# Attention between image columns and rows with the key projection folded into the query, the output bias moved to GpSimd, and image 1's group statistics taken inside image 0's attention

## The chip, the cores and the metric

The kernel runs on one core of one Trainium2 chip. The metric is the device time of one launch in microseconds. The profile is of one execution.

## What is computed

The input x has two images of 256 x 256 positions with 128 channels, in float32. Two layers follow each other, and each adds its result to x. This case concerns layer 0:

```
g   = groupnorm(x)                       # 32 groups of 4 channels, statistics over the whole image
q   = g Wq' + bq ;  k = g Wk' + bk ;  v1 = g Wv1' + bv1 ;  v2 = g Wv2' + bv2
a   = softmax(q k' / sqrt(128))          # queries: column l of the image; keys: row l
x1  = x + ((a v2) * v1) Wo' + bo
```

Attention is separate for each l from 0 to 255: the queries (and v1) are the 256 positions of column l, the keys (and v2) those of row l, and the result belongs to column l. Layer 1 takes x1, normalises it in the same way, and runs a gated depthwise convolution and a selective scan with 256 inner channels and 16 states over all 65,536 positions. It is not touched by the change, and it takes most of the time.

## The kernel before

The kernel has four stages, one after the other.

1. **Start (lines 69 to 184).** Small weights are loaded through SP's queue, transposed by TensorE and copied by ACT.
2. **Statistics (L225 to L243).** For each image, eight pieces of 4 MB (`TT = 64` positions per partition, `NT = 8`) come in through SP's queue into three buffers `xt`; for each piece DVE issues 32 `bn_stats`, one per channel group, over 256 elements. `group_stats` (L187) combines them: 32 `bn_aggr` over the pieces, two small matmuls, and a few small DVE operations and one GpSimd power give the scale `rs` and shift `sh` of each channel. Both images are done before attention begins.
3. **Attention (L255 to L400).** For each image, 16 groups (`NG`) of 16 values of l (`LG`) are loaded, one group ahead of its use: `xc` holds columns for the queries' side, `xr` rows for the keys' side. One call of `attention` handles two values of l (`LQ = 2`), 512 positions, so a group has 8 calls, an image 128, the kernel 256. A call transposes and normalises `xnc` and `xnr` (TensorE, then ACT), computes `q`, `k`, `v1`, `v2` (TensorE; biases added by DVE or ACT on the way out of PSUM), and then for each of its two l: scores `s_ps` (two matmuls), maximum `mx` and `nmx` (DVE), `e` with its sum `den` (ACT), `rden` and `a` (DVE), the transposes `aT_ps`, their copy `aT` (ACT for the first, DVE for the second), and `c_ps` (TensorE). At the end DVE forms `ct`, TensorE the output `o_ps`, and DVE adds `xc` to it into the group's `x1g`. The output's bias is a matmul of one row, `ones_row` x `bo_row`, that opens the accumulation in `o_ps`. After a group, DVE issues 32 `bn_stats` on `x1g` for layer 1's statistics, and POOL's queue stores `x1g` to `x1` in HBM. After an image, `group_stats` combines them.
4. **Scan stage (L402 onwards).** Layer 1, whose order of work is written out by hand in slots.

In the first three stages the order of instructions on each engine is set by the tile framework's scheduler when the program is built[...]. All of `xnc_ps`, `xnr_ps`, `q_ps`, `k_ps`, `v1_ps`, `v2_ps` and `o_ps` take turns in three PSUM buffers:

```
ps_mm = actx.enter_context(tc.tile_pool(name="at_mm", bufs=3, space=PSUM))
```

[...]

Of the kernel before, what the change touches and what calls it, by code (L numbers as in the profile page):

```python
# [8 lines left out]
F32 = mybir.dt.float32  # L9
AF = mybir.ActivationFunctionType  # L10
ALU = mybir.AluOpType
# [4 lines left out]
P = 128  # L16
# [5 lines left out]
def attn_then_ssm_kernel(  # L22
# [26 lines left out]
    nc = tc.nc  # L49
    B, H, W, C = x.shape  # L50
    L = H * W
    G = 32
    CG = C // G
# [4 lines left out]
    TB = 512  # L58
# [10 lines left out]
    def column(name, src):  # L69

        t = const.tile([P, 1], F32, name=name)
        nc.sync.dma_start(out=t, in_=src.rearrange("(p o) -> p o", o=1))
        return t
# [11 lines left out]
    neg_half = const.tile([P, TB // P], F32, name="neg_half")  # L85
    nc.vector.memset(neg_half, -0.5)

    ones_row = const0.tile([1, P], F32, name="ones_row")
    nc.vector.memset(ones_row, 1.0)

    wq = const0.tile([P, P], F32, name="wq")
    wk = const0.tile([P, P], F32, name="wk")
    wv1 = const0.tile([P, P], F32, name="wv1")
    wv2 = const0.tile([P, P], F32, name="wv2")
    wo = const0.tile([P, P], F32, name="wo")
    bq_c = column("bq_c", bq)
    bk_c = column("bk_c", bk)
    bv1_c = column("bv1_c", bv1)  # L100
    bv2_c = column("bv2_c", bv2)
    bo_row = const0.tile([1, TB // P, C], F32, name="bo_row")
    nc.sync.dma_start(out=bo_row, in_=bo.partition_broadcast(TB // P).unsqueeze(0))

    cb_c = columns("cb_c", conv_b)
    dtb_c = columns("dtb_c", dt_b.rearrange("o d -> (o d)"))
# [24 lines left out]
    with tc.tile_pool(name="prep", bufs=1) as prep, tc.tile_pool(  # L131
        name="prep2", bufs=3
    ) as prep2, tc.tile_pool(name="prep_ps", bufs=4, space=PSUM) as prep_ps:
        inp = prep.tile([P, 2 * NH, P], F32, name="inp")
        nc.sync.dma_start(out=inp, in_=in_proj_w.rearrange("(k p) c -> p k c", p=P))
        cw = prep.tile([P, NH, 9], F32, name="cw")
        nc.sync.dma_start(out=cw, in_=conv_w.rearrange("(h p) o i j -> p h (o i j)", p=P))
        outp = prep.tile([P, DI], F32, name="outp")
        nc.sync.dma_start(out=outp, in_=out_proj_w)
        xpw = prep.tile([64, DI], F32, name="xpw")  # L140
        nc.vector.memset(xpw, 0.0)
        nc.sync.dma_start(out=xpw[0:DR, :], in_=x_proj_w[0, 0:DR, :])
        nc.sync.dma_start(out=xpw[32:64, :], in_=x_proj_w[0, DR : DR + 2 * NS, :])
        dtw = prep.tile([P, NH, DR], F32, name="dtw")
        nc.sync.dma_start(out=dtw, in_=dt_w[0].rearrange("(h p) r -> p h r", p=P))
        alog_d = dram.tile([CQ, SR, NCG, NSG], F32, name="alog_d")
        for g in range(NCG):
            for m in range(NSG):
                nc.sync.dma_start(
                    out=alog_d[:, :, g, m],  # L150
                    in_=A_logs[g * CQ : (g + 1) * CQ, m * SR : (m + 1) * SR],
                )
        alog = prep.tile([P, NCG, NSG], F32, name="alog")
        nc.sync.dma_start(out=alog, in_=alog_d.rearrange("c r g m -> (c r) g m"))
        a_pos = prep.tile([P, NCG, NSG], F32, name="a_pos")
        nc.scalar.activation(a_pos, alog, AF.Exp)
        nc.vector.tensor_scalar(a_neg, a_pos, -1.0, None, ALU.mult)

        def transposed(dst, src, n):
            pt = prep_ps.tile([P, P], F32, name="pt")  # L160
            m = dst.shape[0]
            nc.tensor.transpose(pt[0:m, 0:n], src, ident[0:n, 0:n])
            nc.scalar.copy(dst, pt[0:m, 0:n])

        for dst, src in ((wq, Wq), (wk, Wk), (wv1, Wv1), (wv2, Wv2), (wo, Wo)):
            wl = prep2.tile([P, P], F32, name="wl")
            nc.sync.dma_start(out=wl, in_=src)
            transposed(dst, wl, P)
        for h in range(NH):
            for tap in range(9):  # L170
                wt = prep2.tile([P, P], F32, name="wt")
                nc.vector.tensor_scalar(wt, inp[:, h, :], cw[:, h, tap : tap + 1], None, ALU.mult)
                transposed(w_tap[:, h, tap, :], wt, P)
            transposed(w_z[:, h, :], inp[:, NH + h, :], P)
            transposed(w_out[:, h, :], outp[:, h * P : (h + 1) * P], P)
            transposed(w_xp[:, h, :], xpw[:, h * P : (h + 1) * P], 64)
            transposed(w_dt[:, h, :], dtw[:, h, :], P)
            nc.vector.tensor_scalar(d_diag[:, h, :], ident, ds_c[:, h : h + 1], None, ALU.mult)
# [43 lines left out]
        nc.vector.tensor_scalar(sh, cs[:, 0:1], rs, -1.0, ALU.mult, ALU.mult)  # L222
        return rs, sh

    gn0 = []  # L225
    TT = 64
    NT = L // (P * TT)
    with tc.tile_pool(name="st", bufs=2) as stp, tc.tile_pool(
        name="st_x", bufs=3
    ) as stx, tc.tile_pool(name="st_ps", bufs=2, space=PSUM) as st_ps:  # L230
        for b in range(B):
            stats = stp.tile([P, G, NT, 6], F32, name="stats")
            for k in range(NT):
                xt = stx.tile([P, TT, C], F32, name="xt")
                nc.sync.dma_start(
                    out=xt,
                    in_=x_tok[b, k * P * TT : (k + 1) * P * TT, :].rearrange(
                        "(p t) c -> p t c", p=P
                    ),
                )  # L240
                for g in range(G):
                    nc.vector.bn_stats(stats[:, g, k, :], xt[:, :, g * CG : (g + 1) * CG])
            gn0.append(group_stats(stats, stp, st_ps, f"0_{b}"))  # L243

# [4 lines left out]
    NG = W // LG  # L251
    LQ = TB // H
    KT = H // P
    gn1 = []
    with ExitStack() as actx:  # L255
        ap = actx.enter_context(tc.tile_pool(name="at", bufs=2))
        ps_mm = actx.enter_context(tc.tile_pool(name="at_mm", bufs=3, space=PSUM))
        ps_s = actx.enter_context(tc.tile_pool(name="at_s", bufs=2, space=PSUM))
        ps_t = actx.enter_context(tc.tile_pool(name="at_t", bufs=2, space=PSUM))
# [11 lines left out]
        def attention(xc, xr, x1g, q, rs, sh):  # L271
# [3 lines left out]
            xnr = normalised("xnr", [xr[:, l, j, :] for l in ls for j in range(KT)], rs, sh)  # L275

            q_ps = ps_mm.tile([P, TB], F32, name="q_ps", tag="mm")
            nc.tensor.matmul(q_ps, wq, xnc, start=True, stop=True)
            qT = ap.tile([P, TB], F32, name="qT")
            nc.vector.tensor_scalar(qT, q_ps, bq_c, None, ALU.add)  # L280
            k_ps = ps_mm.tile([P, TB], F32, name="k_ps", tag="mm")
            nc.tensor.matmul(k_ps, wk, xnr, start=True, stop=True)
            kT = ap.tile([P, TB], F32, name="kT")
            nc.scalar.activation(kT, k_ps, AF.Identity, bias=bk_c)
            v1_ps = ps_mm.tile([P, TB], F32, name="v1_ps", tag="mm")
            nc.tensor.matmul(v1_ps, wv1, xnc, start=True, stop=True)
            v1 = ap.tile([P, TB], F32, name="v1")
# [12 lines left out]
            for r in range(LQ):  # L300
                own = slice(r * H, (r + 1) * H)
                s_ps = ps_s.tile([P, KT, H], F32, name="s_ps")
                for i in range(KT):
                    nc.tensor.matmul(
                        s_ps[:, i, :],
                        qT[:, r * H + i * P : r * H + (i + 1) * P],
                        kT[:, own],
                        start=True,
                        stop=True,
                    )  # L310
# [41 lines left out]
            ct = ap.tile([P, TB], F32, name="ct")  # L352
            nc.vector.scalar_tensor_tensor(ct, c_ps, bv2_c, v1, ALU.add, ALU.mult)
            o_ps = ps_mm.tile([P, LQ, KT, C], F32, name="o_ps", tag="mm")
            nc.tensor.matmul(o_ps, ones_row, bo_row, start=True, stop=False)
            for r in range(LQ):
                for i in range(KT):
                    t = r * H + i * P
                    nc.tensor.matmul(
                        o_ps[:, r, i, :],  # L360
                        ct[:, t : t + P],
                        wo,
                        start=False,
                        stop=(r == LQ - 1 and i == KT - 1),
                    )
            nc.vector.tensor_tensor(  # L366
                x1g[:, :, q * LQ : (q + 1) * LQ, :],
                o_ps.rearrange("p r i c -> p i r c"),
                xc[:, :, q * LQ : (q + 1) * LQ, :],
                ALU.add,  # L370
            )

        for b in range(B):
            rs, sh = gn0[b]
            stats1 = ap.tile([P, G, NG, 6], F32, name="stats1")

            def load(g):
                ls = slice(g * LG, (g + 1) * LG)
# [12 lines left out]
            for g in range(NG):  # L391
                nxt = load(g + 1) if g + 1 < NG else None
                x1g = ap.tile([P, KT, LG, C], F32, name="x1g")
                for q in range(LG // LQ):
                    attention(*got, x1g, q, rs, sh)
                for gr in range(G):
                    nc.vector.bn_stats(stats1[:, gr, g, :], x1g[:, :, :, gr * CG : (gr + 1) * CG])
                nc.gpsimd.dma_start(  # L398
                    out=x1[b][:, g * LG : (g + 1) * LG, :].rearrange("(i p) l c -> p i l c", p=P),
                    in_=x1g,  # L400
                )
                got = nxt  # L402
            gn1.append(group_stats(stats1, ap, ps_mm, f"1_{b}"))

    front.close()
# [509 lines left out]
```

## Time and profile before

| what | value |
|---|---|
| median of 3 runs | 18009.35 us (18005.79 to 18027.44) |
| profiled execution | 17985.75 us, span 17983.9 us |
| start and statistics | 0 to 240 us |
| attention, image 0 | 253 to 1772 us |
| attention, image 1 | 1800 to 3322 us |
| scan stage, with its prologue | 3345 us to the end |
| busy over the span | PE 79%, DVE 85%, ACT 62%, POOL 75% |
| mean granted TensorE clock | 0.906 |

Shares over the whole span say little here, since more than four fifths of it are the scan stage. The change lies in the first 3,345 us, so each of its steps is read in a window of its own. A matmul of float32 appears as two records[...] with the exception of transposes, which have one.

### The profile page before, as it was taken

To read this page: it belongs to the slowest core of one execution; us is meant where nothing else is said; L and a number is where in the kernel's file an instruction comes from. 1 tells how busy PE (TensorE), PEld (TensorE's weight loads), DVE (VectorE), ACT (ScalarE), POOL (GpSimd) and SP (SyncE) were. 2 spreads that over 40 slices of the span, in tenths; PEclk is the share of its full clock that TensorE was granted. 3 is DMA by queue.
4 is the path that set the end of the run, shared out by engine and by line. 5 is a ranking of instruction groups with operands and counts; after the bars stand their busy time and mean duration, and the time that the engine had idled before them with its cause. 6 is when DMAs were issued, how large, how long until landed. Compare 5 with 4: busy or idle time off the path is not lost. (4 is left out here: it accounts for less than half of the span.)

```text
span 17983.9 us, 178799 instructions
## 1 busy us (share of the span) xinstructions
PE 14262.3 (79%) x56375; PEld 6982.8 (39%) x56375; DVE 15218.5 (85%) x12864; ACT 11112.9 (62%) x19870; POOL 13400.1 (75%) x7084
## 2 busy tenths in 40 slices
PE   4999999777777777777777777777777777777776
PEld 3666666433333333333333333333333333333333
DVE  6555555499999999999999999999999999999998
ACT  2444444466666666666666666666666666666665
POOL 0000000299999999999999999999999999999998
PEclk7999999888899999999999888889888899999887
DMA  4122122266666666666666666666666666666664
GB/s 190 65 71 71 57 71 71 92 220 218 218 221 220 221 221 221 221 221 221 220 220 221 221 219 219 220 220 221 221 220 218 219 221 220 220 220 220 220 219 170
DMA packets 1426641, 3452.04 MB, mean 192 GB/s; under 512 B 119788, under 2 KB 710936, under 8 KB 1407256
## 3 DMA queue, kind: packets, MB, share of 16 engines
q1 hardware_dynamic: 1416984, 3373.49, 54.7%
q0 software_dynamic: 8704, 67.11, 0.9%
q8 instruction: 443, 7.26, 0.2%
q14 instruction: 510, 4.18, 0.1%
HBM read 2752.28 MB, written 687.88 MB: 191 GB/s over the span
## 5 line engine op out<-in xcount | busy, mean ns | idle before, releaser
L787 POOL TENSOR_TENSOR hb<-du_r,bb 128x1024 f32<-128x1024 f32 x4096 | 9566.1, 2360 | 0.0
L794 DVE TENSOR_TENSOR_SCAN da<-da,state,hb 128x1024 f32<-128x1024 f32 x2944 | 6912.4, 2348 | 1064.3 <-ACT da L779 749.3
L779 ACT ACTIVATE da<-delta_r,a_neg 128x1024 f32<-128x1024 f32 x4096 | 4575.5, 1117 | 1155.2 <-DVE hb L794 1086.4
L504 PE MATMUL u_ps<-xn,w_tap 128*128 128x512 f32 x9216 | 4218.6, 603 | 332.3 <-ACT sz L540 242.8
L806 DVE TENSOR_TENSOR yc<-da,cc 128x1024 f32<-128x1024 f32 x2944 | 3605.0, 1225 | 254.2 <-DVE da L794 4.6
L806 POOL TENSOR_TENSOR yc<-hb,cc 128x1024 f32<-128x1024 f32 x1152 | 2714.5, 2356 | 818.9 <-issue 411.9
L794 DVE TENSOR_TENSOR_SCAN hb<-da,state,hb 128x1024 f32<-128x1024 f32 x1152 | 2697.4, 2342 | 15.6 <-ACT da L779 15.3
L826 PE MATMUL y<-yc,sel 128*32 128x512 f32 x16384 | 2469.9, 671 | 280.5 <-POOL yc L806 274.1
L504 PEld LDWEIGHTS u_ps<-xn,w_tap 128*128 128x128 f32 x9216 | 1710.5, 192 | 2348.3 <-issue 1764.8
L398 POOL DMA_DIRECT2D x<-x1g x32 | 23.2, 725 | 3035.0 <-DVE x1g L366 3035.0
L656 PE MATMUL yt<-centre,ys 128*128 128x256 f32 x4096 | 1226.0, 452 | 798.1 <-ACT ob L726 797.0
L799 ACT COPY state<-da 128x1 f32<-128x1 f32 x2944 | 461.2, 157 | 2209.2 <-DVE yc L806 2206.7
L656 PEld LDWEIGHTS yt<-centre,ys 128*128 128x128 f32 x4096 | 895.4, 226 | 1200.8 <-ACT ob L726 992.0
L691 PE MATMUL yd<-ident,yn 128*128 128x128 f32 x2048 | 382.0, 317 | 1126.6 <-ACT yn L680 955.7
L826 PEld LDWEIGHTS y<-yc,sel 128*32 128x32 f32 x16384 | 477.0, 115 | 1973.1 <-issue 1263.9
L552 PE MATMUL xd_ps<-xs,w_xp 128*64 128x512 f32 x1024 | 602.2, 720 | 314.9 <-ACT state L799 174.4
L691 PEld LDWEIGHTS yd<-ident,yn 128*128 128x128 f32 x2048 | 273.3, 160 | 1407.7 <-ACT yn L680 993.9
L570 PE MATMUL dt_ps<-xd,w_dt 8*128 8x512 f32 x1024 | 608.5, 675 | 191.0 <-ACT xd L565 184.1
L515 ACT ACTIVATE xs<-u_ps,cb_c 128x512 f32<-128x512 f32 x512 | 349.6, 683 | 617.8 <-PE u_ps L504 342.5
L318 ACT ACTIVATE e<-s_ps,nmx 128x256 f32<-128x256 f32 x1024 | 472.5, 473 | 355.1 <-DVE nmx L314 354.6
L598 POOL TENSOR_TENSOR xs<-delta,xs 128x1024 f32<-128x1024 f32 x256 | 603.7, 2358 | 40.5 <-ACT delta L589 39.2
L716 PEld LDWEIGHTS o_ps<-w_out,yg 128*128 128x128 f32 x4096 | 604.7, 212 | 35.6
(134 smaller groups left out, 18144.6 us busy)
## 6 DMA issues: line engine op xcount, KB each, us to landing
bb<-bc_d SPq DMA_DIRECT2D x1024, 512.0 KB, 4.2
cc<-bc_d SPq DMA_DIRECT2D x1024, 512.0 KB, 5.2
delta_r<-delta_d SPq DMA_DIRECT2D x1024, 512.0 KB, 5.6
du_r<-du_d SPq DMA_DIRECT2D x1024, 512.0 KB, 4.1
xs_d<-xs SPq DMA_DIRECT2D x128, 1024.0 KB, 3.9
xr<-xs_d SPq DMA_DIRECT2D x256, 512.0 KB, 5.1
delta_d<-delta SPq DMA_DIRECT2D x128, 1024.0 KB, 7.2
du_d<-xs SPq DMA_DIRECT2D x256, 512.0 KB, 3.1
```

Of the source, the lines that this page charges most:

```text
L504: nc.tensor.matmul(o["u"], w_tap[:, h, 3 * dy + dx, :], o["xn"][:, i * RB + dy : i * RB + dy + RB, dx : dx + W], start=(dy == 0 and dx == ...
L552: nc.tensor.matmul(o["xd_ps"], w_xp[:, h, :], o["xs"][:, h, i * TB : (i + 1) * TB], start=(h == 0), stop=(h == NH - 1),)
L570: nc.tensor.matmul(o["dt"], w_dt[:, h, :], o["xd"][0:DR, i * TB : (i + 1) * TB], start=True, stop=True,)
L598: nc.gpsimd.tensor_tensor(du, o["delta"][:, h, :], du, ALU.mult)
L656: nc.tensor.matmul(o["yt"][:, j, :], ys[k, h][:, t0 + j * P : t0 + (j + 1) * P], centre[:, (1 - h) * P : (1 - h) * P + DI], start=(h == 0) ...
L691: nc.tensor.transpose(o["yd"][:, h, j * P : (j + 1) * P], o["yn"][:, j, h * P : (h + 1) * P], ident,)
L716: nc.tensor.matmul(o["o"][:, j, :], o["yg"][:, h, j * P : (j + 1) * P], w_out[:, h, :], start=False, stop=(j == WT - 1 and h == NH - 1),)
L779: nc.scalar.activation(da, spreads["delta", k, h, q], AF.Exp, scale=a_neg[:, g, m : m + 1])
L787: nc.gpsimd.tensor_tensor(hb, spreads["du", k, h, q], repeats["bb", k, h, m], ALU.mult)
L794: nc.vector.tensor_tensor_scan(u["h"], u["da"], u["hb"], st, ALU.mult, ALU.add)
L806: eng.tensor_tensor(u["yc"], u["h"], repeats["cc", k, h, m], ALU.mult)
L826: nc.tensor.matmul(y[q * CQ : (q + 1) * CQ, cols], sel, units[t + q]["yc"][:, cols], start=False, stop=(m == NSG - 1),)
```

## The change

- **One matrix for the scores.** The scores are q k' = (g Wq' + bq)(g Wk' + bk)'. What `bk` adds is the same for all keys of a query, so softmax drops it. The rest is (g Wq'Wk + bq Wk) g'. The kernel computes `wqk` = Wq'Wk and `bqk` = Wk'bq once, at the start. The matmul and the eviction of `k` go; the scores' moving operand is `xnr` itself.
- **Output bias.** The one-row matmul goes. GpSimd writes `xc + bo` into `x1g`, with `bo_all` being the bias on all partitions, and DVE then adds `o_ps` to it in place.
- **Statistics.** Only image 0's are taken before attention, in 16 pieces of 2 MB (`TT = 32`, six buffers). Image 1's pieces are issued by `piece_stats` inside the loop over image 0's groups, into one buffer of a new pool `at1`; `group_stats` for image 1 follows that loop.

```diff
-    wq = const0.tile([P, P], F32, name="wq")
-    wk = const0.tile([P, P], F32, name="wk")
+    wqk = const0.tile([P, P], F32, name="wqk")
+    bqk = const0.tile([P, 1], F32, name="bqk")
...
-    bo_row = const0.tile([1, TB // P, C], F32, name="bo_row")
-    nc.sync.dma_start(out=bo_row, in_=bo.partition_broadcast(TB // P).unsqueeze(0))
+    bo_all = const0.tile([P, C], F32, name="bo_all")
+    nc.sync.dma_start(out=bo_all, in_=bo.partition_broadcast(P))
...
-        for dst, src in ((wq, Wq), (wk, Wk), (wv1, Wv1), (wv2, Wv2), (wo, Wo)):
+        wqr = prep.tile([P, P], F32, name="wqr")
+        nc.sync.dma_start(out=wqr, in_=Wq)
+        wkr = prep.tile([P, P], F32, name="wkr")
+        nc.sync.dma_start(out=wkr, in_=Wk)
+        qk_ps = prep_ps.tile([P, P], F32, name="qk_ps", tag="pt")
+        nc.tensor.matmul(qk_ps, wqr, wkr, start=True, stop=True)
+        nc.scalar.copy(wqk, qk_ps)
+        bqk_ps = prep_ps.tile([P, P], F32, name="bqk_ps", tag="pt")
+        nc.tensor.matmul(bqk_ps[:, 0:1], wkr, bq_c, start=True, stop=True)
+        nc.scalar.copy(bqk, bqk_ps[:, 0:1])
+        for dst, src in ((wv1, Wv1), (wv2, Wv2), (wo, Wo)):
...
-    TT = 64
+    TT = 32
     NT = L // (P * TT)
-    with tc.tile_pool(name="st", bufs=2) as stp, tc.tile_pool(
-        name="st_x", bufs=3
+    def piece_stats(b, k, stats, pool):
+        xt = pool.tile([P, TT, C], F32, name="xt")
+        nc.sync.dma_start(
+            out=xt,
+            in_=x_tok[b, k * P * TT : (k + 1) * P * TT, :].rearrange("(p t) c -> p t c", p=P),
+        )
+        for g in range(G):
+            nc.vector.bn_stats(stats[:, g, k, :], xt[:, :, g * CG : (g + 1) * CG])
+    with tc.tile_pool(name="st", bufs=1) as stp, tc.tile_pool(
+        name="st_x", bufs=6
     ) as stx, tc.tile_pool(name="st_ps", bufs=2, space=PSUM) as st_ps:
...
+        stats = stp.tile([P, G, NT, 6], F32, name="stats")
+        for k in range(NT):
+            piece_stats(0, k, stats, stx)
+        gn0[0] = group_stats(stats, stp, st_ps, "0_0")
...
-            nc.tensor.matmul(q_ps, wq, xnc, start=True, stop=True)
+            nc.tensor.matmul(q_ps, wqk, xnc, start=True, stop=True)
-            nc.vector.tensor_scalar(qT, q_ps, bq_c, None, ALU.add)
-            k_ps = ps_mm.tile([P, TB], F32, name="k_ps", tag="mm")
-            nc.tensor.matmul(k_ps, wk, xnr, start=True, stop=True)
-            kT = ap.tile([P, TB], F32, name="kT")
-            nc.scalar.activation(kT, k_ps, AF.Identity, bias=bk_c)
+            nc.vector.tensor_scalar(qT, q_ps, bqk, None, ALU.add)
...
-                        kT[:, own],
+                        xnr[:, own],
...
-            nc.tensor.matmul(o_ps, ones_row, bo_row, start=True, stop=False)
...
-                        start=False,
-                        stop=(r == LQ - 1 and i == KT - 1),
+                        o_ps[:, r, i, :], ct[:, t : t + P], wo, start=True, stop=True
...
-            nc.vector.tensor_tensor(
-                x1g[:, :, q * LQ : (q + 1) * LQ, :],
-                o_ps.rearrange("p r i c -> p i r c"),
+            to = x1g[:, :, q * LQ : (q + 1) * LQ, :]
+            nc.gpsimd.tensor_tensor(
+                to,
                 xc[:, :, q * LQ : (q + 1) * LQ, :],
+                bo_all.unsqueeze(1).unsqueeze(1).to_broadcast([P, KT, LQ, C]),
                 ALU.add,
             )
+            nc.vector.tensor_tensor(to, o_ps.rearrange("p r i c -> p i r c"), to, ALU.add)
...
+                if b + 1 < B:
+                    for k in range(g * NT // NG, (g + 1) * NT // NG):
+                        piece_stats(b + 1, k, stats0, ap1)
                 got = nxt
+            if b + 1 < B:
+                gn0[b + 1] = group_stats(stats0, ap, ps_mm, f"0_{b + 1}")
```

More of the change, by code (lines that the diff above doesn't have):

```diff
@@ L86, in attn_then_ssm_kernel @@
     nc.vector.memset(neg_half, -0.5)
-    ones_row = const0.tile([1, P], F32, name="ones_row")
-    nc.vector.memset(ones_row, 1.0)
-    wq = const0.tile([P, P], F32, name="wq")
-    wk = const0.tile([P, P], F32, name="wk")
+    wqk = const0.tile([P, P], F32, name="wqk")
+    bqk = const0.tile([P, 1], F32, name="bqk")
     wv1 = const0.tile([P, P], F32, name="wv1")
@@ L98, in attn_then_ssm_kernel @@
     bq_c = column("bq_c", bq)
-    bk_c = column("bk_c", bk)
     bv1_c = column("bv1_c", bv1)
     bv2_c = column("bv2_c", bv2)
-    bo_row = const0.tile([1, TB // P, C], F32, name="bo_row")
-    nc.sync.dma_start(out=bo_row, in_=bo.partition_broadcast(TB // P).unsqueeze(0))
+    bo_all = const0.tile([P, C], F32, name="bo_all")
+    nc.sync.dma_start(out=bo_all, in_=bo.partition_broadcast(P))
     cb_c = columns("cb_c", conv_b)
@@ L159, in transposed @@
         def transposed(dst, src, n):
-            pt = prep_ps.tile([P, P], F32, name="pt")
+            pt = prep_ps.tile([P, P], F32, name="pt", tag="pt")
             m = dst.shape[0]
@@ L223, in group_stats @@
         return rs, sh
-    gn0 = []
-    TT = 64
+    gn0 = {}
+    TT = 32
     NT = L // (P * TT)
-    with tc.tile_pool(name="st", bufs=2) as stp, tc.tile_pool(
-        name="st_x", bufs=3
-    ) as stx, tc.tile_pool(name="st_ps", bufs=2, space=PSUM) as st_ps:
[L231 to L243, printed above, removed]
+    def piece_stats(b, k, stats, pool):
[8 more added lines that the diff above has]
+        name="st_x", bufs=6
+    ) as stx, tc.tile_pool(name="st_ps", bufs=2, space=PSUM) as st_ps:
+        stats = stp.tile([P, G, NT, 6], F32, name="stats")
+        for k in range(NT):
+            piece_stats(0, k, stats, stx)
+        gn0[0] = group_stats(stats, stp, st_ps, "0_0")
     x1 = [dram.tile([H, W, C], F32, name=f"x1_{b}") for b in range(B)]
@@ L256, in attn_then_ssm_kernel @@
         ap = actx.enter_context(tc.tile_pool(name="at", bufs=2))
+        ap1 = actx.enter_context(tc.tile_pool(name="at1", bufs=1))
         ps_mm = actx.enter_context(tc.tile_pool(name="at_mm", bufs=3, space=PSUM))
@@ L359, in attention @@
                     nc.tensor.matmul(
-                        o_ps[:, r, i, :],
-                        ct[:, t : t + P],
-                        wo,
-                        start=False,
-                        stop=(r == LQ - 1 and i == KT - 1),
-                    )
-            nc.vector.tensor_tensor(
-                x1g[:, :, q * LQ : (q + 1) * LQ, :],
-                o_ps.rearrange("p r i c -> p i r c"),
+                        o_ps[:, r, i, :], ct[:, t : t + P], wo, start=True, stop=True
+                    )
+            to = x1g[:, :, q * LQ : (q + 1) * LQ, :]
+            nc.gpsimd.tensor_tensor(
+                to,
                 xc[:, :, q * LQ : (q + 1) * LQ, :],
+                bo_all.unsqueeze(1).unsqueeze(1).to_broadcast([P, KT, LQ, C]),
                 ALU.add,
             )
+            nc.vector.tensor_tensor(to, o_ps.rearrange("p r i c -> p i r c"), to, ALU.add)
         for b in range(B):
             rs, sh = gn0[b]
-            stats1 = ap.tile([P, G, NG, 6], F32, name="stats1")
+            stats1 = ap1.tile([P, G, NG, 6], F32, name="stats1")
+            if b + 1 < B:
+                stats0 = ap1.tile([P, G, NT, 6], F32, name="stats0")
             def load(g):
@@ L401, in attn_then_ssm_kernel @@
                 )
+                if b + 1 < B:
+                    for k in range(g * NT // NG, (g + 1) * NT // NG):
+                        piece_stats(b + 1, k, stats0, ap1)
                 got = nxt
+            if b + 1 < B:
+                gn0[b + 1] = group_stats(stats0, ap, ps_mm, f"0_{b + 1}")
             gn1.append(group_stats(stats1, ap, ps_mm, f"1_{b}"))
```

## The prediction

> **What bounds the kernel now.** The windows view cuts the span at the stages: attention of image 0, the gap between the images, attention of image 1, and the scan stage. Its columns are the stretch, then busy time and instruction count of PE, weight loads, DVE, ACT and POOL, then the granted TensorE clock, the DMA share and GB/s.
>
> ```profile
> 253.00:1772.00 1519.00, 1476.55 (x7155) 1000.68 (x7156) 865.12 (x2270) 743.62 (x1791) 10.99 (x15) 0.99 0.19 67
> 1772.00:1800.00 28.00, 4.88 (x20) 3.79 (x20) 23.11 (x72) 0.00 (x0) 0.72 (x1) 0.50 0.40 150
> 1800.00:3322.00 1522.00, 1476.78 (x7166) 999.78 (x7165) 868.59 (x2283) 744.36 (x1792) 12.07 (x17) 0.99 0.17 60
> 3500.00:17983.00 14483.00, 11176.94 (x41762) 4925.49 (x41761) 13244.08 (x7550) 9572.63 (x16204) 13352.88 (x7023) 0.90 0.64 218
> ```
>
> The diff touches nothing in the last row, and the built programs issue that stage in the same order, so I cost it at nothing. In attention TensorE is busy 97%, DVE 57%, POOL not at all. The timeline inside attention shows why TensorE stays busy:
>
> ```profile
> 1510.23 1.13 PE L345 MATMUL c_ps<-aT,v 128*128 128x256 f32 x4
> ...
> 1516.75 0.66 PE L266 MATMUL xnc_ps<-ident,xc 128*128 128x128 f32 x4
> ...
> 1518.69 1.04 PE L278 MATMUL q_ps<-xnc,wq 128*128 128x512 f32 x2
> ...
> 1521.71 1.13 PE L345 MATMUL c_ps<-aT,v 128*128 128x256 f32 x4
> ```
>
> One attention (one call, two values of l) takes 1521.71 - 1510.23 = 11.48 us. While its softmax runs on DVE and ACT, TensorE transposes the next one's xnc and xnr and computes its q, k, v1. Array time: in the scan stage's prologue successive 512-column records start 0.43 us apart, so 128 columns cost 0.107 us. An attention holds 96 such units (xnc 4, xnr 4, q 8, k 8, v1 8, v2 8, scores 16, aT 8, c 16, bias 8, o 8) = 10.24 us of its 11.48.
>
> The last attention of image 1 has no successor to overlap with. Its timeline is the key view:
>
> ```profile
> 3308.47 1.89 PE L304 MATMUL s_ps<-kT,qT 128*128 128x256 f32 x8
> ...
> 3312.30 0.72 PE L336 MATMUL aT_ps<-ident,a 128*128 128x128 f32 x4 [0.89 <-DVE a L330]
> ...
> 3313.75 1.13 PE L345 MATMUL c_ps<-aT,v 128*128 128x256 f32 x4
> ...
> 3315.77 1.13 PE L345 MATMUL c_ps<-aT,v 128*128 128x256 f32 x4 [0.78 <-DVE aT L341]
> ...
> 3317.75 1.98 PE L359 MATMUL o_ps<-wo,ct 128*128 128x128 f32 x8 [0.84 <-DVE ct L353]
> ...
> 3319.77 0.69 DVE L366 TENSOR_TENSOR x1g<-o_ps,xc 128x512 f32<-128x512 f32 x1 [2.08 <-PE o_ps L359]
> ```
>
> The reader is to see TensorE waiting for DVE three times, and o taking 1.98 us where 1.09 is usual: the clock had halved.
>
> [...] in attention the clock halves at 361.98, 457.5 and 553.1 us, 28 windows apart, each time after a group's DVE statistics, and the image's tail shows
>
> ```profile
> 1764.86:1768.27 3.41, 2.08 (x11) 0.99 0.01 2
> 1768.27:1771.69 3.42, 2.64 (x7) 0.50 0.00 0
> ```
>
> [...] I count units: 128-row columns per window against what full rate could do. Full clock was followed by half at 0.30 (1764.86) and 0.36 (3314.51), and stayed at 0.44 (3311.10). A half-rate window went back to full at 0.79 of itself and above, and stayed half at 0.83 and below. All of this fits one threshold near 0.40 of full rate. The one-row bias matmul does not count: the window from 358.57 has 0.60 with it, 0.35 without, and halved. [...]
>
> **The change part by part.**
>
> *Start.* Before: 512 statistics instructions at 168.2 us busy, 64 aggregations at 15.0 and small steps fill DVE from 51.7 to 236.1.
>
> ```profile
> L242 DVE BATCH_NORM_STATS2 stats<-xt 128x6 f32<-128x256 f32 x512 | 168.2, 423 | 1.6 <-PE pt L162 1.6
> ```
>
> After: 512 of half the size for image 0. The same shape is L397, whose 32 take 6.29 us (0.197 each): 100.7. The 32 aggregations are over 96 values, 14.4 us in the gap at 1782. With 2 us of image 1's first piece that DVE issues in between: 51.7 + 117 = 169. The 33.5 MB come at the 390 GB/s of the 60 to 100 us window in 86 us, done before 130, so DVE still decides. **-67 us.** Weights: two matmuls instead of two transposes, under 1 us, ahead of a DVE that is busy anyway: nothing.
>
> *Work off TensorE.* k and bias: 16 units, 1.71 us per attention; ACT loses kT (0.69). Alone, 256 x 1.71 = 437 us, since TensorE binds.
>
> *What moves.* The built program's instruction order says otherwise. Before, TensorE issues o(n)'s bias, xnc, xnr, q, k, v1 of n+1 between the scores and o of n. After, with the early bias matmul gone, the order is o(n), xnc, xnr, q, v1, v2, scores, aT, c, o of n+1, in both images; and q(n+1) also waits for DVE's x1g of n. TensorE never runs ahead; every softmax is waited out, as in the tail above. One period from its durations: scores to o 3317.75 - 3308.47 = 9.28; o 0.86; xnc 0.43; 0.26 to ACT's start, normalise 0.78, 0.05 to q (row 353.30 to 354.82 of the timeline); q, v1, v2 2.57. Sum **14.2 us**, TensorE loaded 8.53. x1g (o's end + 0.27 + 0.69) and qT (q's start + 1.08 + 0.75) are ready before their users.
>
> *Clock.* Times from the scores' start: scores to 1.7, aT near 3.8 to 4.4 and 4.7 to 5.2, c 5.3 to 6.2 and 7.3 to 8.1, o and transposes 9.3 to 11.0, q to 14.2. A window that begins 0.3 to 2.4 us after the start holds under 0.40 (2.1 of 3.41: 6 in 10), one at 5.9 to 6.4 as well (1.5 in 10). After the first kind three windows stay half (0.69, 0.68 loaded, then 0.93), which doubles c, c, o and the transposes on the path: 17.4 us. After the second one window: 15.3. Mean 0.6 x 17.4 + 0.15 x 15.3 + 0.25 x 14.2 = **16.3 us**.
>
> *Group ends (30).* DVE issues the 32 statistics of x1g (6.3 us) between x1g and the next qT, whose slack is 1.7: +4.6, and TensorE's idling makes a half-rate stretch over the scores sure: I take +8 (4.6 at full clock).
>
> *Image 1's statistics.* DVE issues all 16 pieces and their aggregation within the first 25 attentions, mostly where it waits; single ones (0.2 us) precede nmx or a: about 0.8 us for each, **+20**; none to 60. SP issues each piece ahead of later loads, with a wait on DVE, but a load has a group's time (over 100 us) of slack.
>
> *GpSimd's add.* 128x512, half of L787's 2360 ns: 1.2 us in 14, long before DVE needs it: nothing[...]. It precedes the stores on POOL's queue, which are free.
>
> *Sum.* 127 x 2 periods x 16.3 = 4140, groups 240, statistics 20, two tails and the gap between the images as now (13.2 + 30.6 + 12.0 = 56): 4456 from the first scores to the last x1g, against 3320.5 - 258.7 = 3062. **+1394 - 67 = +1327.** The profiled execution took 17985.75 us (span 17983.9), 24 below the median of 18009: **19,310 us**.
>
> **Rivals.** *The clock holds.* If the load that counts is more than my units, periods are 14.2, groups 4.6: 3607 + 138 + 20 + 56 = 3821, +692: 18,680. For it: 0.36 to 0.44 is a bracket, and my windows sit near it. Against: the tails halved both times. *Half clock is stickier.* At a threshold of 0.42, or with 0.2 us more per wait, the mean with groups goes from 17.3 to about 17.9: 19,540. *Faster: TensorE stays the bound.* If q, v1 of n+1 got ahead of o(n), the 437 us would be saved with the 67, less 20: about 17,500. It decides at a period under 11.6 us (3062 + 67 - 20 - 56 - 30 x 3.4 of today's group ends, over 254); the order read from the built program speaks against it, since TensorE's matmuls run in program order in every stretch I read. *Image 1's statistics aren't hidden:* their 101 us would add 80 to any case.
>
> **How the numbers follow.** Main case 0.70, sticky 0.12, clock holds 0.15, faster 0.03. The range reaches from the held clock to the sticky case. A measurement of this kernel can tell about 0.2% from no change. Faster 0.03, same 0.01, slower 0.96.
>
> **What would show it.** Right: attention ends near 4,650 us instead of 3,320; PE busy in attention falls well under 90% with a mean clock near 0.8; periods mix 14 to 18 us; PE waits for DVE a, aT, ct and ACT xnc each period; the start ends near 175 us; the scan stage keeps its length. Wrong: xnc of the next attention ahead of aT, or a clock near 1.0 in attention.

## The result and the profile after

The kernel after takes 19465.49 us (median of 4 runs, 19464.44 to 19469.21) against 18009.42 for the kernel before beside it: a ratio of **1.0807, interval 1.0788 to 1.0825**. The forecast was 19,310 us in a range of 18,670 to 19,560, so sign and size came out; the single terms did not all. The profiled execution has a span of 19462.3 us, against 17983.9.

| stretch, from the profiles | before, us | after, us | difference | forecast |
|---|---|---|---|---|
| to the first scores | 258.7 | 175.9 | -82.8 | -67 |
| first scores to the end of the last x1g | 3061.8 | 4601.9 | +1540 | +1394 |
| the rest | 14663.4 | 14684.5 | +21 | 0 |

The windows view of after, cut at the stages as it was for before (PE, weight loads, DVE, ACT and POOL busy, then clock, DMA share, GB/s):

```profile
176.00:2445.00 2269.00, 1697.50 (x6543) 1169.76 (x6542) 1042.27 (x2755) 671.47 (x1637) 170.75 (x143) 0.77 0.15 57
2490.00:4778.00 2288.00, 1717.88 (x6662) 1181.73 (x6662) 958.55 (x2299) 681.27 (x1664) 156.99 (x133) 0.77 0.11 40
4960.00:19461.00 14501.00, 11248.50 (x41760) 4980.86 (x41758) 13244.41 (x7548) 9569.65 (x16203) 13343.56 (x7021) 0.89 0.63 218
```

Read the two attention rows against those of before. TensorE was busy 97% at a clock of 0.99; now it is busy 75% at 0.77, and DVE (46% and 42%) and ACT (30%) are less busy as well. No engine is the bound any more: the stage has become a chain of waits. One period of it, in the timeline of after (PE alone):

```profile
3006.61 1.89 PE L312 MATMUL s_ps<-xnr,qT 128*128 128x256 f32 x8
3010.34 1.86 PE L344 MATMUL aT_ps<-ident,a 128*128 128x128 f32 x7 [1.85 <-DVE a L338]
3012.00 2.00 PE L353 MATMUL c_ps<-aT,v 128*128 128x256 f32 x4
...
3015.00 1.13 PE L353 MATMUL c_ps<-aT,v 128*128 128x256 f32 x4 [0.78 <-DVE aT L349]
3016.98 1.16 PE L366 MATMUL o_ps<-wo,ct 128*128 128x128 f32 x8 [0.84 <-DVE ct L361]
...
3019.44 1.12 PE L290 MATMUL q_ps<-xnc,wqk 128*128 128x512 f32 x2 [0.43 <-ACT xnc L280]
...
3022.15 1.03 PE L312 MATMUL s_ps<-xnr,qT 128*128 128x256 f32 x4
```

From scores to scores 15.54 us pass. The brackets are the four waits that the forecast named, and nothing of the next attention fills them. The first c takes 2.00 us where the second takes 1.13 for the same four records: half clock. The granted clock in the trace of after has two values, 1.00 and 0.50, in 1,518 stretches, and each of these but the last, where the record ends, lasts a whole number of times 3.413 us to within 2 ns (before has the same two values in 924 stretches, all of such lengths). A piece of that length is called a window here. Those around this period show when the clock changes (PE busy, clock, DMA share, GB/s):

```profile
2997.35:3000.76 3.41, 1.78 (x10) 1.00 0.00 0
3000.76:3004.17 3.41, 3.39 (x16) 0.50 0.00 0
3004.17:3007.58 3.41, 3.41 (x17) 1.00 0.02 5
3007.58:3011.00 3.42, 1.57 (x9) 1.00 0.00 0
3011.00:3014.41 3.41, 3.16 (x10) 0.50 0.00 0
```

Each of the two windows with a long wait (busy 1.78 and 1.57 us of 3.41) is followed by one at half rate. Busy time holds more than array work: a record of the scores lasts 0.38 us at full rate, and the next starts 0.216 us after it. Counted as the prediction counts, the window from 3007.58 holds the last 0.74 us of the scores and four transposes of 0.107 us: 1.17 of 3.41, or 0.34 of full rate. From 400 to 4700 us, the waits of TensorE are these (us in total, times, longest):

```profile
PE aT_ps L344 <- DVE a L338: 536.3, 310, 5.0
PE o_ps L366 <- DVE ct L361: 202.7, 239, 1.7
PE c_ps L353 <- DVE aT L349: 186.6, 238, 0.8
PE s_ps L312 <- DVE qT L292: 90.2, 30, 3.7
```

In before, from 300 to 3300 us, the first three come to 3.9 us together (2.3, 0.8 and 0.8). The fourth has a count of 30: once for each group end, where DVE issues the 32 statistics of x1g ahead of the next qT.

Taken from ct to ct, attentions inside a group last 16.90 us on average (224 of them; 19 under 14.6, the least 14.45; 53 from there to 16.5; 152 above), those across a group end 25.18 (30), and the one across the images 42.5. In before the same three are 10.90, 18.83 and 43.3.

### The profile page after: what moved, and what is told of

Its sections match the earlier page's. It is cut to its first block, busy times and chain, and to the rows that moved or that the text cites. A ratio compares the mean times of both kernels' runs of the same rounds, so it can differ in the third digit from the quotient of the medians.

```text
span 19462.3 us, 177469 instructions
## 1 busy us (share of the span) xinstructions
PE 14820.0 (76%) x55353; PEld 7404.5 (38%) x55353; DVE 15428.9 (79%) x13375; ACT 10986.6 (56%) x19614; POOL 13712.1 (70%) x7340
## 5 line engine op out<-in xcount | busy, mean ns | idle before, releaser
L405 POOL DMA_DIRECT2D x<-x1g x32 | 23.9, 746 | 4057.1 <-DVE x1g L376 3932.8
L280 ACT ACTIVATE xnc<-xnc_ps,sh,rs 128x512 f32<-128x512 f32 x256 | 198.9, 777 | 2168.0 <-PE xnc_ps L278 2168.0
L353 PE MATMUL c_ps<-aT,v 128*128 128x256 f32 x2048 | 878.5, 573 | 203.7 <-DVE aT L349 200.7
L344 PE MATMUL aT_ps<-ident,a 128*128 128x128 f32 x2048 | 554.3, 367 | 590.1 <-DVE a L338 576.4
L564 PE MATMUL xd_ps<-xs,w_xp 128*64 128x512 f32 x1024 | 554.8, 669 | 283.6 <-ACT state L811 143.2
```

The costliest lines, as they stand in the source:

```text
L344: nc.tensor.transpose(aT_ps[:, j, i * P : (i + 1) * P], a[:, i, j * P : (j + 1) * P], ident)
L353: nc.tensor.matmul(c_ps[:, own], v2[:, r * KT + j, :], aT[:, j, :], start=(j == 0), stop=(j == KT - 1),)
L564: nc.tensor.matmul(o["xd_ps"], w_xp[:, h, :], o["xs"][:, h, i * TB : (i + 1) * TB], start=(h == 0), stop=(h == NH - 1),)
```

## The experiments

Ten kernels ran, each with the kernel before beside it. The ratio is to that one.

| label | what it is | median, us | ratio, interval |
|---|---|---|---|
| gpsimd_bias_alone | before + output bias on GpSimd | 19546.8 | 1.0861, 1.0845 to 1.0877 |
| bias_back | after, bias on TensorE as before | 17813.8 | 0.9897, 0.9880 to 0.9913 |
| opener | after + a one-column matmul into o_ps | 17745.5 | 0.9861, 0.9846 to 0.9876 |
| own_buffer | after, o_ps in a PSUM pool of its own | 17611.2 | 0.9784, 0.9769 to 0.9798 |
| fill | after + two filler matmuls | 18987.2 | 1.0551, 1.0535 to 1.0567 |
| order_control | fill without the fillers | 19423.7 | 1.0791, 1.0773 to 1.0809 |
| stats_back | after, statistics ahead again | 19491.5 | 1.0829, 1.0813 to 1.0845 |
| wqk_alone | before + Wq'Wk | 17878.3 | 0.9934, 0.9919 to 0.9949 |
| opener_spread | opener, x1g's statistics spread | 17689.6 | 0.9830, 0.9815 to 0.9845 |
| own_spread | own_buffer, x1g's statistics spread | 17514.1 | 0.9733, 0.9717 to 0.9749 |

### Which edit does it: gpsimd_bias_alone and bias_back

```diff
# gpsimd_bias_alone, against before
-            nc.tensor.matmul(o_ps, ones_row, bo_row, start=True, stop=False)
...
+            nc.gpsimd.tensor_tensor(to, xc[...], bo_all..., ALU.add)
+            nc.vector.tensor_tensor(to, o_ps.rearrange("p r i c -> p i r c"), to, ALU.add)
```

bias_back is the kernel after with this edit undone.

> The kernel before with only the output bias moved to GpSimd; k, its eviction and the statistics ahead of attention stay. Theory: serial order with k in it, shortest period 14.5 + 0.9 = 15.4 us, mean with half clock and group ends near 18.7: about 19,700 us, slower than the changed kernel. Rival B: 18,000 us, as before. Rival A: between 18,100 and 19,500 us, with TensorE's order still overlapped.

> The changed kernel with the output bias as a one-row matmul again, and no add on GpSimd; Wq'Wk and the moved statistics stay. Theory: overlapped order, TensorE carries 9.39 us per attention, period about 10.6 us: 256 x 0.85 and the start's 80 below the kernel before, about 17,750 us. Rival A says about the same, with GpSimd gone. Rival B: stays at 19,300 us or more.

One edit of the three carries the whole loss: alone it costs 8.6%, and without it the other two gain 1.0%. gpsimd_bias_alone came out some 150 us under its expected 19,700, and bias_back 64 us above its 17,750 (wqk_alone below shows why). In gpsimd_bias_alone k is still computed, and TensorE waits for the same tiles as in after:

```profile
PE aT_ps L334 <- DVE a L328: 564.0, 339, 3.8
PE o_ps L356 <- DVE ct L351: 211.2, 250, 0.8
```

Its mean period inside groups, 17.0 us, is close to the 16.9 of after, although it has 0.86 us more array work in each. That work is not free: its periods without a half-rate window last 15.31 us, those of after 14.45. But half of its periods have none: they alternate between 15.31 us and about 18.8 us, and the mean clock from 400 to 4700 us is 0.84, against 0.77 in after. Two such periods last 34.1 us, as long as ten of the clock's windows of 3.413 us. So do, within 0.1 us, 144 of the 160 pairs of successive periods that touch no group end. In after it is four periods that often make 20 windows, as shown further below, which gives the same five windows for one attention.

### Is it GpSimd, or the place of o_ps: opener and own_buffer

```diff
# opener, against after
             o_ps = ps_mm.tile([P, LQ, KT, C], F32, name="o_ps", tag="mm")
+            nc.tensor.matmul(
+                o_ps[:, 0, 0, 0:1], ident[0:1, :], ident[0:1, 0:1], start=True, stop=True
+            )
```
```diff
# own_buffer, against after
-        ps_mm = actx.enter_context(tc.tile_pool(name="at_mm", bufs=3, space=PSUM))
+        ps_mm = actx.enter_context(tc.tile_pool(name="at_mm", bufs=2, space=PSUM))
+        ps_o = actx.enter_context(tc.tile_pool(name="at_o", bufs=1, space=PSUM))
...
-            o_ps = ps_mm.tile([P, LQ, KT, C], F32, name="o_ps", tag="mm")
+            o_ps = ps_o.tile([P, LQ, KT, C], F32, name="o_ps")
```

> The changed kernel plus one matmul of a single column that opens o_ps where the bias matmul used to; its result is overwritten, and GpSimd's add stays. Theory (the early claim on o_ps let TensorE run ahead; without it each softmax is waited out): the overlapped order is back, TensorE carries 8.53 us per attention, the period falls to 9.8 to 10.5 us and the clock in attention is above 0.95: 17,450 to 17,650 us. Rival A (GpSimd's add holds DVE up or comes late): 19,200 us or more. Rival B (image 1's statistics on DVE are what costs): 19,200 us or more.

> The kernel after with one change of buffers and no other: o_ps gets a PSUM pool of its own (one buffer), and the pool that xnc, xnr, q, v1 and v2 share has two instead of three, so PSUM holds as much as before. No matmul is added. In the built program the next attention's xnc, xnr, q, v1, v2 and part of its scores now stand between this one's scores and o, as in the kernel opener. Theory (o_ps took its place in the shared rotation only when its first writer could issue, after ct, and held the next attention's tiles behind it): TensorE overlaps again, the period is that of opener less the opening matmul's 0.31 us at most, mean 11.0 to 11.3, clock over 0.95: 17,650 to 17,760 us. Rival A: it was the opening matmul's own work, not the place of o_ps: then about 19,450 as after. Rival B: with two shared buffers q or v1 waits for a buffer to be evicted (0.7 us each): mean near 12, about 17,950.

Both keep GpSimd's add, and both are faster than before, so the add is not what costs. opener's gain fell short of the expected 17,450 to 17,650 by about 100 us: its periods reach 10.15 us, but across a group end it needs 18 to 20 us and then 7 to 8, and its mean is 11.28. own_buffer adds no instruction to TensorE and gives PSUM no more room, yet it gains 2.2%, more than expected. Its timeline (PE) shows the order:

```profile
2407.91 1.12 PE L291 MATMUL q_ps<-xnc,wqk 128*128 128x512 f32 x2 [0.43 <-ACT xnc L281]
2408.87 0.60 PE L345 MATMUL aT_ps<-ident,a 128*128 128x128 f32 x4
2409.31 1.02 PE L295 MATMUL v_ps<-xnc,wv 128*128 128x512 f32 x2
2410.20 1.13 PE L354 MATMUL c_ps<-aT,v 128*128 128x256 f32 x4
2411.17 0.60 PE L345 MATMUL aT_ps<-ident,a 128*128 128x128 f32 x4
2411.60 1.06 PE L302 MATMUL v_ps<-wv,xnr 128*128 128x128 f32 x8
2412.55 1.13 PE L354 MATMUL c_ps<-aT,v 128*128 128x256 f32 x4
2413.52 1.46 PE L313 MATMUL s_ps<-xnr,qT 128*128 128x256 f32 x6
2414.81 1.05 PE L367 MATMUL o_ps<-wo,ct 128*128 128x128 f32 x8
...
2417.61 1.12 PE L291 MATMUL q_ps<-xnc,wqk 128*128 128x512 f32 x2 [0.43 <-ACT xnc L281]
```

q, v1 and v2 of the next attention stand between aT and c of this one, and its scores ahead of this one's o. The period is 9.70 us with one wait of 0.43. Over the two attention stages:

```profile
176.00:1550.00 1374.00, 1210.10 (x6636) 922.07 (x6635) 992.84 (x2789) 663.17 (x1662) 171.77 (x144) 1.00 0.26 97
1610.00:2950.00 1340.00, 1181.04 (x6510) 903.30 (x6508) 888.12 (x2289) 649.60 (x1624) 151.18 (x128) 0.99 0.19 70
```

So the loss hung on where o_ps takes its turn. In the trace of after, all 255 later attentions have their xnc behind the o of the one before (in that of before a single one has, the first of image 1); either edit alone undoes this. The reading that fits both: in the shared rotation of three buffers the first writer decides. With a matmul that needs no ct, o_ps has its buffer early and the next attention's tiles may follow; without one, o_ps comes after ct, and xnc, xnr, q, v1 and v2 behind it wait for it in the built order. How the scheduler arrives at its order was not looked at; this is inferred from the two edits. It matters which tiles share a rotation: three buffers in one rotation with o_ps took 19,465 us, two and one apart 17,611.

### What the half clock costs: fill and order_control

```diff
# fill, against after: the scores of both l first, then fillers, then both softmaxes
+            for _ in range(2):
+                nc.tensor.matmul(c_ps, wv1, xnc, start=True, stop=True)
```

The fillers are overwritten by c. order_control has `range(0)`.

> The changed kernel, its order still serial, with two matmuls of 512 columns after the scores that fill TensorE's wait (1.7 us of extra work per attention; their result is overwritten in c_ps, and both l's scores are written ahead of both softmaxes). Theory (half clock takes some 2.5 us of the 17 us period, and a window of the softmax wait triggers it): clock in attention above 0.9, most periods 14.5 us, about 18,850 us. Rival C (the clock matters little, the chain of waits is all): 19,450 us; Rival D (TensorE's work is on the path): 256 x 1.7 more, 19,900 us.

> The control for the run fill: the kernel after with the scores of both l issued ahead of both softmaxes, as fill has them, and no filler matmul. If the filler matmuls are what raised the clock, this one is as the kernel after: 19,465 us within 0.3%, clock near 0.77 in attention. Rival: the restructuring by itself gave fill its 478 us: near 18,990 or below, as the two filler matmuls cost up to 0.9 us at full clock that this kernel does not have (0 to 220 us).

order_control is after to within the intervals, so the rearrangement does nothing that can be measured. Two matmuls more in each attention, 1.7 us of array work, make the kernel some 430 us faster than without them (0.024 in the ratio): they stand where TensorE waits for the softmax, and the clock over attention is higher. The order is otherwise that of after: xnc still follows the o of the attention before, and the shortest period is 14.45 us in both. The windows view of fill over attention has a clock of 0.92, where the two attention rows of after have 0.77; over the whole of the profiled executions it is 0.897 for fill and 0.867 for order_control:

```profile
200.00:4200.00 4000.00, 3228.78 (x13846) 2117.82 (x13844) 1951.80 (x5008) 1302.44 (x3207) 324.14 (x273) 0.92 0.15 56
```

Inside groups 146 of 224 periods are under 14.6 us, the mean is 14.95 instead of 16.90; group ends still take 24.4. Its 18,987 us are 137 above the expected 18,850. What remains above before, some 980 us, is the serial order with the half clock that the fillers leave, most of it at group ends.

### The other two edits: stats_back and wqk_alone

stats_back puts both images' statistics ahead of attention in the form of before. wqk_alone is before with k dropped and `wqk`, `bqk` in place.

> This is the kernel after with both images' statistics taken ahead of attention again, as in the kernel before; TensorE's order stays serial. Theory (the prediction's step): the statistics of the second image cost about 20 us inside the first image's attention and their move shortened the start by 83 us, so putting them back costs 83 - 20 = +63: about 19,530 us, with the first scores near 258 us and the attention stage about 20 us shorter than after's 4602. Rival A: they delay DVE by their whole busy time of about 100 us in a serial attention, where DVE is on the path in most periods; then the kernel is 20 us faster than after: about 19,445. Rival B: they also upset the clock, and attention shortens by over 150 us: under 19,400.

> This is the kernel before with k dropped and q formed with Wq'Wk, and nothing else: bias matmul and statistics stay as in before, and the program's order on TensorE overlaps as in before. If TensorE's array work alone sets the period, as the prediction's 437 us for k and the bias took it, half of that is saved, 256 x 0.856 = 219 us: about 17,785 us. Rival: bias_back (this edit and the move of the statistics) saved 190 us of which the shorter start is 83, so k's matmul is worth only about 107 plus the 20 that the second image's statistics cost, because the period is then set by waits of q for ACT's xnc and by the softmax: about 17,880, with a period near 11.1 to 11.3 us and PE busy below 97%.

In the two profiles the move of the statistics is worth 75.3 us at the start (first scores at 251.2 in stats_back, 175.9 in after) and costs 41.5 us in attention (4560.4 and 4601.9). The run times differ by 0.0022 in the ratio, some 40 us, with intervals that overlap, so they cannot tell the net of +34 from nothing or from the expected +63. The 41.5 us are not firm either: attention in order_control, with the statistics where after has them, is 25 us shorter than in after.

wqk_alone came out at the rival's 17,880, half of what array work alone would give. Its steady period is 11.32 us against 11.48, though k's matmul stood for 0.86. A group of eight attentions is 3.4 us shorter than in before, and 2.6 us of this come from the three periods that follow a group's end. The timeline and the waits say why the steady period gains so little:

```profile
677.01 1.24 PE L344 MATMUL aT_ps<-ident,a 128*128 128x128 f32 x5 [0.51 <-DVE a L338]
```
```profile
PE aT_ps L344 <- DVE a L338: 81.1, 158, 1.6
```

With k gone, TensorE reaches aT before the softmax is done and waits 0.51 us, 158 times. In before this wait came to 2.3 us in all.

### Versions that beat both: opener_spread and own_spread

```diff
                 for q in range(LG // LQ):
                     attention(*got, x1g, q, rs, sh)
-                for gr in range(G):
-                    nc.vector.bn_stats(stats1[:, gr, g, :], x1g[...])
+                    if g > 0:
+                        for gr in range(q * G // 8, (q + 1) * G // 8):
+                            nc.vector.bn_stats(stats1[:, gr, g - 1, :], x1p[...])
+                x1p = x1g        # the last group's statistics follow the loop
```

> The kernel opener (after, with a one-column matmul that opens o_ps early) in which the 32 statistics of a group's x1g are taken four after each attention of the next group, those of the last group at its end. In the built program scores of the next attention now stand between c and o of this one, and v1 and v2 between the aT transposes. Theory: the group ends of opener (18 to 20 us and then 7 to 8, about 4 us more than two periods, 30 of them) go, and with them the halved windows they bring: 120 us less at least, about 17,620. If the period, 10.15 us at best in opener, also comes nearer the array's 80 units, 8.53 us, as the deeper overlap would let it (mean 10.3 instead of 11.28): 254 x 1.0 = 250 us less, about 17,490. Rival: four statistics (0.8 us of DVE) in each attention lie ahead of a qT or an a and lengthen each period by up to 0.8: 254 x 0.8 = 200 us more against 120 saved, about 17,830.

> own_buffer and the statistics of x1g spread four by four over the next group's attentions, as in opener_spread. If both gains stand beside each other: own_buffer less the 56 us that the spread gave to opener, about 17,600 to 17,700 us, below both kernels and below opener_spread (17,690). If two shared buffers cost what the opening matmul cost: level with opener_spread within 0.3%.

The spread gave opener 56 us, less than the 120 expected: the long period of each group shrinks from about 19 us to about 13.6, but the steady period stays at 10.15. To own_buffer it gives 97 us, which puts own_spread below its expected 17,600 to 17,700. own_spread is the fastest kernel of this study, 2.7% below before. Its mean from ct to ct is 10.38 us against 10.75 in own_buffer, and own_buffer's 20.5 and 23.9 us at the group ends of image 0 are gone.

## Why the prediction was right, and which terms were off

- **The serial order: right.** TensorE's busy share, the mean clock and the four waits are as forecast, and own_buffer and opener show that the order carries the loss. The forecast read the order from the built program and named the missing bias matmul; the runs add the reason, the place of o_ps in the rotation.
- **The walked period, 14.2 us: 0.25 short.** The least measured is 14.45. From o's start to the next scores it is 5.17 us (2709.71 to 2714.88 in the timeline of after) where the walk had 4.95: o takes 0.99 until xnc starts, not 0.86, and q, v1, v2 take 2.71, not 2.57.
- **The clock: half rate after thinly loaded windows right, shares wrong.** The mean inside groups is 16.90 instead of 16.3, which over 224 periods makes 134 us, most of the miss. The threshold "near 0.40" was not at fault. Counted as the forecast counts (0.107 us for each record's 128 columns, twice that at half rate, one-row matmuls not at all; successive records of the scores, 256 columns each, start 0.216 us apart at 1.00 and 0.427 at 0.50), from 2600 to 3000 us of after all 26 full-rate windows loaded 0.39 or less were followed by half rate, and all 32 loaded 0.41 or more stayed. The harmful places were near the forecast's too: windows that begin 0.6 to 2.6 us after the scores' start, where it had 0.3 to 2.4, or 6.0 to 6.3 us after it, where it had 5.9 to 6.4. What failed is the step from these places to chances of 0.6, 0.15 and 0.25, which takes windows to begin evenly over the period. Of the 192 periods that touch no group end, 169 (88%) had a window of the first kind, 10 of the second, and 13 (7%) neither. Period and window fall into step:

```profile
2953.96 1.89 PE L312 MATMUL s_ps<-xnr,qT 128*128 128x256 f32 x8
2971.97 1.89 PE L312 MATMUL s_ps<-xnr,qT 128*128 128x256 f32 x8
2989.76 1.89 PE L312 MATMUL s_ps<-xnr,qT 128*128 128x256 f32 x8
3006.61 1.89 PE L312 MATMUL s_ps<-xnr,qT 128*128 128x256 f32 x8
3022.15 1.89 PE L312 MATMUL s_ps<-xnr,qT 128*128 128x256 f32 x8
```

  These four periods, each with a window of the first kind, last 68.19 us, and 20 windows 68.27, so the next four meet the windows at the same places. Of the 96 runs of four such periods in after, 52 are within 0.3 us of this. The costs were off the other way: a window of the first kind brings one, two or three half-rate windows (15.6, 16.9 or 18.0 us), 17.1 us on average, not always three and 17.4. With the measured shares the forecast's costs would give a mean of 17.1 us, where 16.9 was measured: the two errors cancel in part, and that much of the hit is luck. The rival "half clock is stickier" has the measured mean with groups, 17.9 (4541 us over 254), but not the cause: no threshold of 0.42 shows. By the forecast's own sum that mean gives 19,310 + 254 x 0.6 = 19,462; the 19,540 written for it does not follow.
- **Group ends, +8 us: right.** 25.18 - 16.90 = 8.3; TensorE waits for qT at 30 of them.
- **The start, -67 us: too small.** It was -82.8. The statistics gave 75.3, and the weights, costed at nothing, 7.5 (stats_back and wqk_alone both start their scores at 251 us, before at 258.7): with that edit DVE starts its statistics earlier, at 44.5 us in wqk_alone against 51.7. Whether the two fewer transposes or the loads before them do this was not separated.
- **Image 1's statistics, +20 us: the size fits, but is not settled.** Image 0 takes 22 us longer than image 1 in after and 20 us in order_control, where stats_back shows 7 between them, so some 15 us; the two profiles against each other give 41, with the doubt named above.
- **GpSimd's add, nothing: no cost shows.** One takes 1.26 us in after; opener and own_buffer keep it and are faster than before; a small cost under their gains is not excluded.
- **k and bias, 437 us "alone, since TensorE binds": too large.** wqk_alone gained 114 us of its 219. In the steady period TensorE was the bound by a margin of only 0.16 us (11.48 to 11.32); the softmax is next. The faster rival's 17,500 would not have come from the two edits in the order of before either: bias_back and opener stayed at 17,814 and 17,745.
- **The scan stage, nothing: right.** The rest after the last x1g is 14,654 to 14,710 us in the profiles of the experiments, and both kernels lie inside.

## What to carry to other kernels

Before an instruction that opens an accumulation is removed, ask which buffer it claims, and what stands behind that buffer in a shared rotation: a tile whose first writer is late should not share one with tiles that are wanted early. An engine that is 97% busy may have another chain right behind it (here the period went from 11.48 to 11.32 us for 0.86 us of array work), so price removed work only up to the next wait. Where TensorE has to wait, see what its clock does: here 1.7 us of filler in each attention went with a clock of 0.92 instead of the 0.77 of after and some 430 us less, and the next attention's work in that place, in own_buffer, with 0.99 to 1.00. In a loop that waits, do not take the clock's windows as evenly spread: the period fell into step with them here, and 88% of the periods met one of the first kind, where the forecast's even spacing had 60%.

## What was not expected of the hardware

- Adding 1.7 us of matmuls to each period of 16.9 made the kernel some 430 us faster (18,987 against 19,424). A window did not have to be idle to be followed by half rate: all 26 full-rate windows with a load of up to 0.39 in the count above were.
- One load very nearly fits the changes in both directions. In the same count the half-rate windows went back to full at 0.75 of their own rate and above, which is 0.375 of full rate (all 25), and stayed half at 0.73 and below (all 34). The forecast's figures for this, back at 0.79 and above, half at 0.83 and below, overlap and fix no threshold. Over 300 to 2900 us of before and after, "a load of 0.375 of full rate or more is followed by full rate, a smaller one by half" is right for 1,501 of 1,522 windows, and the loads of the other 21 lie between 0.35 and 0.39.
